# Attention scores behind all of q: three in a row, the third in the banks of the results, with the last outer product's inner products in another order

## The chip, the core and the metric

The kernel runs on one core of a Trainium2 chip. The metric is the time of one execution on the device in microseconds (us); lower is better. TensorE (PE) multiplies matrices, VectorE (DVE) adds and evicts sums, ScalarE (ACT) takes the exponentials and copies, and the DMA queues move data. Matmul results land in PSUM[...].

## The reference

Two layers of the same form on an input of 8 images, 512 channels and 32 x 32 positions (S = 1024), all in float32. Each layer is a group norm, projections to q, k and v, attention with 8 heads of 64 channels, a projection of the result and the addition of the input:

```python
xn = group_norm(x, 8 groups) * gamma + beta
q, k, v = (W_qkv @ xn + b_qkv), split into 8 heads of 64 channels
attn = softmax(q . k / 8)             # 1024 x 1024 for each head
out = x + W_p @ (attn . v) + b_p
```

## The kernel before

The work is 16 jobs, one image in one layer each, taken in pairs of images. For each job TensorE computes v, then (mixed with the output projection of the job before) k and q, and then the attention. All queues are in the order in which the Python code emits the instructions. A planner clock (`advance`, `later`) decides where transfers and other small steps are slotted in.

**Projections.** The projections of q, k and of the result are products of 2 x 2 blocks computed with seven products instead of eight, and this twice, one level inside the other. The outer level has seven outer products for each projection, in the order `OUTER = (1, 2, 6, 5, 7, 3, 4)`; each of them is again seven inner products of 128 x 128 by 128 x 256, in the order `ORDER = (1, 5, 6, 2, 7, 3, 4)`. The function `chain` holds one outer product. It uses four banks, z, y, u and w (their names rotate, so a bank called vd in a profile can be the z of its chain):

- product 1 starts z, which ScalarE copies to y; product 5 starts w, which ScalarE copies to `s5` in SBUF
- product 6 adds onto z, and ScalarE copies z to u (line 413)
- product 2 adds onto y, which ScalarE evicts (line 605, or 603 without a bias)
- product 7 adds onto z, and VectorE evicts z plus `s5` (line 609, or 607)
- product 3 adds onto u, which VectorE evicts in the same way
- product 4 adds onto z, and ScalarE evicts z (line 605, or 603)

So product 7 must come behind the copy to u, and product 4 behind product 7's eviction.

`deep_phases` makes one thunk for each inner product and interleaves neighbouring outer products: outer product c begins when the one before it is at its inner product 7, and from there the two alternate. The last outer product has nobody behind it, so its last four thunks follow each other. Each outer product uses four banks, by turns the left and the right half of PSUM; the last one has the right half. Behind the evictions of products 7 and 3 one waiting outer addition (line 622, 128 x 1024) or another small step is put into VectorE's queue.

**Attention.** A job has 8 groups (four pairs of heads, two halves of the positions) of 8 steps (blocks of 128 keys), 64 steps in all. In a step, `scores` multiplies k and q on the four 64 x 64 quarters of the array into two banks (`sc`, line 764), and ScalarE takes the exponential of 128 x 1024 numbers (line 769). VectorE adds the exponentials up (`add`, lines 779 and 781). `values` multiplies the exponentials with v into two other banks (`po`, line 795). Values run `LEAD = 2` steps behind the scores. The left half of PSUM holds two `sc` tiles, the right half two `po` tiles.

**From the projections to attention.** When all but the last two inner products of q's last outer product are issued, the left half of PSUM is given to `sc`, and scores 0 and 1 are issued; then the last two inner products (3 and 4) follow, and the right half is given to `po`. Then `run` goes on with score 2, values 0, score 3, values 1 and so on. This place occurs 16 times, once for each job.

Of the kernel before, what the change touches and what calls it, by code (L numbers as in the profile page):

```python
# [33 lines left out]
LEAD = 2  # L34
# [5 lines left out]
K, V, Q, O = range(4)  # L40
FACTOR = {1: A11, 2: A12, 3: S4, 4: A22, 5: S1, 6: S2, 7: S3}
ORDER = (1, 5, 6, 2, 7, 3, 4)
OUTER = (1, 2, 6, 5, 7, 3, 4)
QT = HALF // 2
RING = 7
# [25 lines left out]
def fast_path(  # L71
# [37 lines left out]
    def advance(us):  # L109
        clock[0] += us  # L110
        due = sorted((t for t in todo if t[0] <= clock[0]), key=lambda t: t[0])
        for t in due:
            todo.remove(t)
            t[1]()

    def banks(half, use):

        if half in ps:
            ps.pop(half)[0].__exit__(None, None, None)
        turns[0] += 1  # L120
        guard = tc.tile_pool(
            name=f"ps{half}_{turns[0]}", bufs=2 if use == "two" else 1, space=PSUM,
            side=("left", "right")[half], reuse_waits="tile",
        )
        ps[half] = (guard, guard.__enter__())

    def two_banks(tag, name):
        return ps[0 if tag == "sc" else 1][1].tile([P, 2, HALF], F32, tag=tag, name=name)
# [235 lines left out]
    def right(src, t, o):  # L364

        if o in (4, 5, 6):
            return t[:, {5: 0, 6: 1, 4: 2}[o]]
        rows = 0 if o in (1, 7) else 2
        cols = slice(0, HALF) if o in (1, 2) else slice(HALF, S)
        return src[:, rows : rows + 2, cols]  # L370
# [112 lines left out]
    def sums_of_four(r, slots):  # L483

        def blk(a, b):
            return r[:, a, b * QT : (b + 1) * QT]

        def first():  # L490
            nc.vector.tensor_sub(slots[0], blk(0, 1), blk(0, 0))
            nc.vector.tensor_sub(slots[1], blk(1, 1), slots[0])

        def second():
            nc.vector.tensor_sub(slots[2], blk(1, 1), blk(0, 1))
            nc.vector.tensor_sub(slots[3], blk(1, 0), slots[1])

        return first, second

    class OutputSums:  # L500
# [6 lines left out]
        def steps(self, c):  # L507
            def first():
# [16 lines left out]
                self.at[c] = slots  # L525
                self.pair = sums_of_four(right(self.src, to[0], OUTER[c]), slots)
                self.pair[0]()
# [3 lines left out]
    def deep_phases(n, extra, outs=None, early=()):  # L531
# [4 lines left out]
        dst = {}  # L536
        chains = [(which, o) for which in ((O, K, Q) if outs else (K, Q)) for o in OUTER]
        tiles = {}
# [4 lines left out]
        def begin(c):  # L543
            which, o = chains[c]
            m = job(which)
            b, layer = jobs[m]
            if o == OUTER[0] and which != O:
                name = "k" if which == K else "q"
# [140 lines left out]
        live, parts = {}, {(0, 0): 2, (0, 1): 3, (1, 1): 2, (1, 0): 2}  # L689
        soon, outer = deque(early), deque()  # L690

        def thunk(c, j):
            def go():
                if j == 0:
                    live[c] = begin(c)
                live[c](ORDER[j])
                if ORDER[j] in (7, 3):
                    if soon:
                        soon.popleft()()
                    elif outer:  # L700
                        outer.popleft()()
                    elif extra and extra[0][0] <= c:
                        extra.popleft()[1]()
                if j == 6:
                    end(c)
                    if c + 1 == len(chains):
                        while outer:
                            outer.popleft()()
                advance(0.43)

            return go
# [32 lines left out]
    class Attention:  # L744
# [6 lines left out]
            self.steps = [(g, kc) for g in range(len(self.groups)) for kc in range(NT)]  # L751
            self.es, self.acc, self.po = {}, {}, {}

        def scores(self, i):
            n, q, k = self.n, self.q, self.k
            groups, steps, es = self.groups, self.steps, self.es
            g, kc = steps[i]
            hp, sh = groups[g]
            sc = two_banks("sc", f"sc_{n}_{i}")
            for h in range(2):  # L760
                for j in range(2):
                    r = slice(j * HD, (j + 1) * HD)
                    k0 = kc * P + h * HD
                    nc.tensor.matmul(  # L764
                        sc[h * HD : (h + 1) * HD, j, :], k[r, hp, k0 : k0 + HD],
                        q[r, hp, sh * HALF : (sh + 1) * HALF], start=True, stop=True,
                    )
            e = epool.tile([P, 2, HALF], F32, tag="e", name=f"e_{n}_{i}")
            nc.scalar.activation(e, sc, AF.Exp, scale=SCALE)  # L769
            es[i] = e  # L770
            if i > 1:
                self.add(i)

        def add(self, i):
# [102 lines left out]

        def run(self, chores):

            steps = self.steps  # L880
            self.add(1)
            for i in range(2, len(steps) + LEAD):
                if i < len(steps):
                    self.scores(i)
                self.values(i - LEAD)
                g, kc = steps[i - LEAD]
                if kc == NT - 1:
                    self.finish(g)
                    advance(0.85)
                if i in chores:  # L890
                    chores[i]()
                advance(1.71)
# [56 lines left out]
    def extend_plan(n):  # L949
        plan.extend((n, V, o) for o in ORDER)  # L950
        plan.extend((n - 1, O, o) for o in ORDER)
        plan.extend((n, which, o) for which in (K, Q) for o in OUTER)

# [148 lines left out]
    def first_plan():  # L1102
        plan.extend((0, which, o) for which in (K, Q) for o in OUTER)
        for _ in range(RING):
# [15 lines left out]
    reads, steps = norm_steps(1)  # L1120
    for n in range(-1, len(jobs)):
        last = n + 1 == len(jobs)
        outs = None
        if n >= 0:
            chores = {}

            def put(i, fn):
                while i in chores:
                    i += 1
                chores[i] = fn  # L1130

            if last:
                w = plain_weights(n)
            else:
                if n == 0:
                    first_factors(put, [(O, 0), (V, 1)])
                elif n == 1:
                    first_factors(put, [(K, 1), (Q, 1)])
                elif n == 2:
                    first_factors(put, [(O, 1)])  # L1140
                for i, (_, fn) in enumerate(extra):
                    put(2 + i, fn)
                at = (10, 19, 22, 24, 26, 28, 36, 39, 42, 45)
                if n == 0:
                    for i, fn in zip((3, 3, 4, 5, 6, 8, 10, 11, 12, 13, 15), reads):
                        put(i, fn)
                    at = (22, 30, 34, 35, 37, 38, 41, 44, 47, 50)
                for i, fn in zip(at, steps + sums(n + 1)):
                    put(i, fn)
                deep_first = deep_steps(n + 1)  # L1150
                for at, fn in zip((52, 54, 57, 59), deep_first[4:]):
                    put(at, fn)
                put(61, lambda: (extend_plan(n + 1), [fetch() for _ in range(RING)]))
            assert max(chores, default=0) < NT * len(att.groups)
            att.run(chores)
            banks(0, "one")
            banks(1, "one")
            if last:
                advance(100.0)
                advance(100.0)  # L1160
                judge()
                plain_proj(n, w)
                break
            outs = OutputSums(n)
            out_sums(n, outs)
            first = v_phase(n + 1, ORDER)
            for thunk in first[:-1]:
                thunk()
            rest = first[-1:]
            extra = deque()  # L1170
            if jobs[n][1] == 1 and jobs[n][0] + 2 < B:
                extra.append((11, lambda b=jobs[n][0] + 2: (x_tile(b), load_x(b))))
            if n == 1:
                load, bias_steps = make_out_bias(1)
                extra.append((8, load))
                extra.extend((11, fn) for fn in bias_steps)
            if n + 2 < len(jobs):
                reads, steps = norm_steps(n + 2)
                extra.extend((15, fn) for fn in reads)
        both = deep_phases(n + 1, extra, outs, deep_first[:4] if outs else ())  # L1180
        both[0]()
        rest[0]()
        if n < 0:
            later(22.0, lambda: load_x(1))
        for thunk in both[1:-2]:
            thunk()
        banks(0, "two")
        att = Attention(n + 1)
        att.scores(0)
        att.scores(1)  # L1190
        for thunk in both[-2:]:
            thunk()
        banks(1, "two")

    for half in (1, 0):
        ps.pop(half)[0].__exit__(None, None, None)
# [246 lines left out]
```

## Time and profile before

| | |
|---|---|
| time, median of three runs | 3218.36 us (3215.56 to 3218.5) |
| span of the profiled run | 3213.6 us |
| PE, DVE, ACT busy | 99%, 86%, 59% of the span |
| scores, PE L764 | 27% of the chain that ended last |
| values, PE L795 | 26% |
| exponential, ACT L769 | 1024 times 1023 ns |
| sum of exponentials, DVE L781 | 768 times 1219 ns |
| a job, from its first score to that of the next | 198.20 us |

A line of the timeline has the start in us from the span's beginning, the duration, the engine, the line of the kernel, the operation, the tile written and the tiles read, the shapes and how many instructions were merged; in brackets the idle time before it and who ended it. Each float32 inner product appears as two matmuls, each score and each values block as eight. Matmuls overlap, so the distance of two starts, and not the duration, is the price of one.

### The profile page before, as it was taken

How to read it: one execution, taken by the hardware profiler on the slowest of the kernel's cores; microseconds unless marked ns; L12 is line 12 of the kernel's file. 1: busy time of each engine (PE TensorE's matmuls, PEld its weight loads, DVE VectorE, ACT ScalarE, POOL GpSimd, SP SyncE). 2: the span in 40 equal slices, each digit the busy share in tenths (PEclk: the TensorE clock that was granted, in tenths of full speed). 3: DMA queues.
4: the chain of work that ended last, by engine and by line, in shares of the span. 5: the costliest groups of instructions: out<-in, count | busy, mean ns of one | idle time of the engine just before them, and what ended most of it. 6: DMA issues, size and time to landing. Idle time of an engine off the chain costs nothing.

```text
span 3213.6 us, 57636 instructions
## 1 busy us (share of the span) xinstructions
PE 3194.8 (99%) x22870; PEld 1850.2 (58%) x22870; DVE 2767.3 (86%) x3958; ACT 1902.4 (59%) x3038; POOL 99.4 (3%) x93
## 2 busy tenths in 40 slices
PE   9999999999999999999999999999999999999999
PEld 7366384563836638365483754837557374573843
DVE  8897998979889798897978889888897888988876
ACT  4746646466565665656656565565656656566563
POOL 0000000000000000000000000000000000000000
PEclk9999999999999999999999999999999999999999
DMA  8234272350613305033160421505216051150501
GB/s 317 96 105 129 68 213 69 93 168 22 210 27 90 89 28 158 22 105 128 31 210 15 119 67 38 147 16 144 93 45 192 16 142 43 55 130 22 173 22 42
DMA packets 149462, 313.04 MB, mean 97 GB/s; under 512 B 33864, under 2 KB 46784, under 8 KB 148160
## 3 DMA queue, kind: packets, MB, share of 16 engines
q1 hardware_dynamic: 132320, 276.77, 26.8%
q0 software_dynamic: 16864, 32.51, 6.2%
q8 instruction: 181, 2.97, 0.4%
q14 instruction: 97, 0.79, 0.1%
HBM read 224.35 MB, written 51.18 MB: 86 GB/s over the span
## 4 chain that ended last, share of the span: by engine, by line
PE 93%; DVE 5%; DMA 1%; issue 1%; ACT 0%; SPq 0%; POOL 0%; DVEq 0%
PE sc L764 27%; PE po L795 26%; PE vd L593 10%; PE zd L593 10%; PE z L462 6%; PE ud L593 4%; PE yd L593 4%; PE v L462 2%; PE y L462 2%; PE u L462 2%; DVE acc L781 1%; PE pp L733 1%; DMA x<-p 0%; DMA w<-wqkv_dram 0%; DVE w L154 0%
## 5 line engine op out<-in xcount | busy, mean ns | idle before, releaser
L769 ACT ACTIVATE e<-sc 128x1024 f32<-128x1024 f32 x1024 | 1045.9, 1023 | 582.4 <-PE sc L764 485.9
L764 PE MATMUL sc<-q,k 64*64 64x512 f32 x8192 | 1061.7, 590 | 0.0
L795 PE MATMUL po<-e,v 64*64 64x512 f32 x8192 | 1057.1, 589 | 0.0
L781 DVE TENSOR_TENSOR acc<-acc,e 128x1024 f32<-128x1024 f32 x768 | 936.3, 1219 | 57.8 <-ACT e L769 9.3
L795 PEld LDWEIGHTS po<-e,v 64*64 64x64 f32 x8192 | 313.0, 133 | 566.0 <-issue 557.5
L764 PEld LDWEIGHTS sc<-q,k 64*64 64x64 f32 x8192 | 309.7, 133 | 559.1 <-issue 545.4
L593 PE MATMUL vd<-deep,w 128*128 128x256 f32 x900 | 252.6, 380 | 1.4 <-DVE p L609 1.3
L779 DVE TENSOR_TENSOR acc<-e,e 128x1024 f32<-128x1024 f32 x128 | 156.4, 1222 | 111.3 <-ACT e L769 111.3
L593 PE MATMUL zd<-deep,w 128*128 128x256 f32 x892 | 248.4, 380 | 3.7 <-DVE p L607 2.0
L593 PEld LDWEIGHTS vd<-deep,w 128*128 128x128 f32 x900 | 170.6, 190 | 26.4 <-DVE p L609 2.5
L593 PEld LDWEIGHTS zd<-deep,w 128*128 128x128 f32 x892 | 168.9, 190 | 29.2 <-DVE p L607 3.3
L811 DVE TRANSPOSE_TENSOR_REDUCE r<-acc 128x32 f32<-128x1024 f32 x128 | 158.5, 1238 | 0.5
L636 POOL DMA_DIRECT2D x<-p x62 | 74.6, 1203 | 1971.5 <-ACT p L603 1408.9
L593 PE MATMUL vd<-os,w 128*128 128x256 f32 x420 | 118.1, 380 | 1.6 <-DVE p L609 1.5
L622 DVE TENSOR_TENSOR p<-p,p 128x1024 f32<-128x1024 f32 x94 | 114.2, 1215 | 0.0
L462 PE MATMUL z<-w,t 128*128 128x256 f32 x480 | 110.9, 379 | 0.0
L462 PE MATMUL z<-w,xn 128*128 128x256 f32 x480 | 110.1, 382 | 0.0
L413 ACT COPY ud<-vd 128x256 f32<-128x256 f32 x173 | 61.8, 357 | 77.2 <-PE vd L593 69.8
L611 ACT COPY s<-zd 128x256 f32<-128x256 f32 x173 | 64.5, 373 | 71.8 <-PE zd L593 71.7
L475 ACT COPY v<-z 128x512 f32<-128x512 f32 x32 | 18.7, 585 | 148.5 <-PE z L462 148.5
L462 PEld LDWEIGHTS z<-w,xn 128*128 128x128 f32 x480 | 90.0, 190 | 23.8 <-issue 12.2
L413 ACT COPY ud<-zd 128x256 f32<-128x256 f32 x156 | 55.7, 357 | 76.6 <-PE zd L593 75.1
(213 smaller groups left out, 4058.7 us busy)
## 6 DMA issues: line engine op xcount, KB each, us to landing
w<-deep SPq DMA_DIRECT2D x287, 448.0 KB, 3.9
w<-keep SPq DMA_DIRECT2D x129, 256.0 KB, 2.7
x<-p POOLq DMA_DIRECT2D x62, 512.0 KB, 6.9
rb<-rd SPq DMA_DIRECT2D x96, 256.0 KB, 4.1
deep<-w SPq DMA_DIRECT2D x42, 448.0 KB, 4.0
x<-x_dram SPq DMA_DIRECT2D x28, 512.0 KB, 4.6
out_dram<-x SPq DMA_DIRECT2D x28, 512.0 KB, 6.2
keep<-raw SPq DMA_DIRECT2D x5, 1792.0 KB, 7.6
```

The source lines that it names most:

```text
L413: nc.scalar.copy(u, z)
L462: nc.tensor.matmul(ps[:, ti * CH : (ti + 1) * CH], r[:, cc, t0 : t0 + P], w[:, cc, :], start=(start and ti == 0 and cc == 0), stop=(cc == ...
L593: nc.tensor.matmul(ps, lhs[:, FACTOR[i], :], moving[i], start=start, stop=True, skip_group_check=True,)
L611: return chain(product, lambda ps: nc.scalar.copy(s5, ps), put, z, y, u, w)
L622: outer.append(lambda: nc.vector.tensor_add(to_, a, b))
L636: nc.gpsimd.dma_start(to_, p(part), accum_op=ALU.add)
L764: nc.tensor.matmul(sc[h * HD : (h + 1) * HD, j, :], k[r, hp, k0 : k0 + HD], q[r, hp, sh * HALF : (sh + 1) * HALF], start=True, stop=True,)
L769: nc.scalar.activation(e, sc, AF.Exp, scale=SCALE)
L779: nc.vector.tensor_add(acc[g], self.es[i - 1], e)
L781: nc.vector.tensor_add(acc[g], acc[g], e)
L795: nc.tensor.matmul(po[g][j * HD : (j + 1) * HD, h, :], v[r, kc, d0 : d0 + HD], e[r, j, :], start=(kc == 0), stop=(kc == NT - 1),)
L811: nc.vector.tensor_reduce(self.r[:, 0, m, :], self.acc.pop(g).rearrange("p j (b e) -> p (j b) e", e=RP), AX.X, ALU.add, apply_transpose=True,)
```

## The change

The two products of q that stood behind scores 0 and 1 are put in front of them. After q is complete, three scores are issued in a row. The left half of PSUM has room for two, so the third takes the first of the two `po` tiles in the right half, and `run` begins with values 0 and goes on with score 3. TensorE then changes only once from products of 128 rows to products of 64 rows, where it changed there, back and there again.

With the scores gone from between product 7 and product 4, the last outer product gets an order of its own, `LAST_ORDER`, which moves product 7 in front of product 2. All other outer products keep `ORDER`.

```diff
+LAST_ORDER = (1, 5, 6, 7, 2, 3, 4)
...
-                live[c](ORDER[j])
-                if ORDER[j] in (7, 3):
+                order = LAST_ORDER if c + 1 == len(chains) else ORDER
+                live[c](order[j])
+                if order[j] in (7, 3):
...
-        def scores(self, i):
+        def scores(self, i, tag="sc"):
...
-            sc = two_banks("sc", f"sc_{n}_{i}")
+            sc = two_banks(tag, f"sc_{n}_{i}")
...
-            if i > 1:
+            if i > 2:
                 self.add(i)
...
             self.add(1)
-            for i in range(2, len(steps) + LEAD):
+            self.add(2)
+            self.values(0)
+            if 2 in chores:
+                chores[2]()
+            for i in range(3, len(steps) + LEAD):
...
-        for thunk in both[1:-2]:
+        for thunk in both[1:]:
             thunk()
         banks(0, "two")
         att = Attention(n + 1)
         att.scores(0)
         att.scores(1)
-        for thunk in both[-2:]:
-            thunk()
         banks(1, "two")
+        att.scores(2, "po")
```

## The prediction

> **What bounds the kernel now.** I read the page first, for the busy engine and for the chain that ended last.
>
> ```profile
> PE 3194.8 (99%) x22870; PEld 1850.2 (58%) x22870; DVE 2767.3 (86%) x3958; ACT 1902.4 (59%) x3038; POOL 99.4 (3%) x93
> ...
> PE 93%; DVE 5%; DMA 1%; issue 1%; ACT 0%; SPq 0%; POOL 0%; DVEq 0%
> ```
>
> TensorE is busy 99% of the span and carries 93% of the chain. So only two things count: how densely TensorE's instructions follow one another, and whether one of them waits. The windows by stage say the same of one job, from its first score to the next job's:
>
> ```profile
> 888.90:1087.10 198.20, 198.20 (x1434) 115.93 (x1433) 170.70 (x237) 119.25 (x192) 6.22 (x5) 1.00 0.29 78
> ```
>
> PE is busy 198.20 of 198.20 us at a granted clock of 1.00. The change touches the place where a job's projections end and its attention begins, 16 times in a run. I read one of them in the timeline, first TensorE alone (start, duration, instruction):
>
> ```profile
> 887.05 0.59 PE L593 MATMUL vd<-deep,w 128*128 128x256 f32 x2
> 887.48 0.59 PE L593 MATMUL zd<-deep,w 128*128 128x256 f32 x2
> 887.92 0.59 PE L593 MATMUL yd<-t,w 128*128 128x256 f32 x2
> 888.35 0.59 PE L593 MATMUL vd<-deep,w 128*128 128x256 f32 x2
> 888.87 1.95 PE L764 MATMUL sc<-q,k 64*64 64x512 f32 x16
> 890.75 0.70 PE L593 MATMUL ud<-t,w 128*128 128x256 f32 x2
> 891.29 0.59 PE L593 MATMUL vd<-deep,w 128*128 128x256 f32 x2
> 891.81 1.09 PE L764 MATMUL sc<-q,k 64*64 64x512 f32 x8
> 892.72 1.04 PE L795 MATMUL po<-e,v 64*64 64x512 f32 x8
> 893.58 0.61 PE L764 MATMUL sc<-q,k 64*64 64x512 f32 x4
> ```
>
> By the chain's order these are: product 6 of q's last outer product, product 4 of the one before it, then products 2 and 7 of the last, scores 0 and 1, products 3 and 4, score 2, values 0. (In the last outer product the bank named vd is the running sum z.) Starts count here, since durations overlap. Products follow at 0.43 us, a score or a values block takes 0.86 (892.72 to 893.58). From product 2 at 887.92 to values 0 at 892.72 are 4.80 us; four products and three scores at these rates would be 4 x 0.432 + 3 x 0.859 = 4.30. The other 0.50 is at the changes of shape and nowhere else. All 16 such places have the same spacing, within 0.01 us.
>
> Then VectorE and ScalarE in the same stretch:
>
> ```profile
> 886.39 0.48 DVE L609 SCALAR_TENSOR_TENSOR p<-zd,bias_step,s 128x256 f32<-128x256 f32 x1 [0.53 <-PE zd L593]
> 886.79 1.22 DVE L622 TENSOR_TENSOR p<-p,p 128x1024 f32<-128x1024 f32 x1
> 887.92 0.48 DVE L609 SCALAR_TENSOR_TENSOR p<-ud,bias_step,s 128x256 f32<-128x256 f32 x1
> 888.32 1.22 DVE L622 TENSOR_TENSOR q<-p,p 128x1024 f32<-128x1024 f32 x1
> 889.45 0.48 DVE L609 SCALAR_TENSOR_TENSOR p<-vd,vec_sb,s 128x256 f32<-128x256 f32 x1
> 889.85 1.22 DVE L622 TENSOR_TENSOR q<-q,p 128x1024 f32<-128x1024 f32 x1
> ```
>
> ```profile
> 887.68 0.36 ACT L413 COPY ud<-vd 128x256 f32<-128x256 f32 x1 [0.49 <-PE vd L593]
> 888.12 0.47 ACT L605 ACTIVATE p<-zd,bias_step 128x256 f32<-128x256 f32 x1
> ```
>
> The 889.45 line is the eviction of product 7. Product 7 was issued at 888.35, and its eviction starts 1.1 us later because VectorE has no gap from 886.39 on: two evictions and two additions of 1.22 us stand ahead of it. In the kernel before this delay is free, because scores 0 and 1 lie between product 7 and product 4.
>
> **What the Trainium skill says.** "TensorEngine Tiling (Array Packing)", Key Properties: a change of tiling mode drains TensorE. The trace agrees and gives the price: going from 128-row products to 64-row scores costs 0.09 at once and 0.05 more after the first half of the score, 0.14 us; going back costs 0.11 and then 0.11 more before product 3's second half, 0.21 us. "PSUM — Partial Sum Buffer", Engine vs sequencer instructions: ScalarE's and VectorE's queues are strict FIFO, and matmuls start and complete in program order. The VectorE lines above agree. "TensorE: Matmul & The Clock Gate", Part 2: weight loads are pulled ahead of running matmuls. After a wait there is nothing to hide the load behind, and the trace shows that too, in the first job's outer products:
>
> ```profile
> 74.54 0.48 DVE L609 SCALAR_TENSOR_TENSOR p<-zd,vec_sb,s 128x256 f32<-128x256 f32 x1
> ...
> 75.07 0.70 PE L593 MATMUL zd<-deep,w 128*128 128x256 f32 x2 [0.93 <-DVE p L609]
> ...
> 75.61 0.59 PE L593 MATMUL yd<-xn,w 128*128 128x256 f32 x2
> ```
>
> The product that waits for an eviction starts 0.05 us after it ends (74.54 + 0.48 = 75.02, then 75.07), and the next follows at 0.54 instead of 0.43: a wait costs 0.11 on top of its length.
>
> **The change part by part.**
>
> *Scores moved behind all of q.* It removes one trip from products to scores and back: 0.14 + 0.21 = 0.36 us saved at each place (0.358 with the third digit kept).
>
> *Product 7 before product 2.* It now follows directly on the other outer product's product 4, at 887.92 if nothing held it. It adds onto z, and must not start before ScalarE has copied z to u: 887.68 + 0.36 = 888.04, so 888.10 with the 0.05. That is 0.18 of waiting and 0.11 for the load. Behind it on TensorE is everything else: product 2 at 888.63, product 3 at 889.07, product 4 due at 889.50.
>
> *Product 4 without the scores in front.* It adds onto z again, so it has to wait until product 7's eviction has read z. The four lines of VectorE's queue ahead of that eviction (outer sums and evictions of the outer product before) depend on nothing that moves, and their order is the same in both kernels. So the eviction again runs from 889.45 to 889.93; product 7 itself is done long before. Product 4 starts at 889.98, 0.48 later than due. Since this wait ends at a time that VectorE sets, it swallows the wait of product 7: the end is the same whether that one happens or not.
>
> *From there on.* Product 4 takes 0.54 after its wait, the change of shape 0.09: score 0 at 890.61. Two scores in a row take 1.77 (1.88 from 888.87 to 890.75, less the 0.11 of the way back): score 2 at 892.38, values 0 at 893.24. Before it was 892.72. The loss is 0.52 us at each place; with the third digit my sum over the 16 places is 8.3 us.
>
> *The third score in a results bank, and the waits this adds.* Score 2 needs two banks that the last outer product used, values 0 the other two, and values 0 also the first exponential. The eviction of product 3 follows the 889.85 addition and ends at about 891.5; that of product 4, on ScalarE, starts some 0.4 us after its second half and ends at about 891.2; both are ahead of 892.38. The exponential of score 0 starts 1.16 us after the score (888.87 to 890.03), so at 891.77, and ends at 892.79, ahead of 893.24. Scores 3 and 4 find their banks free since values 0 and 1 have already waited for the same exponentials. One more waiting instruction on TensorE's queue finds its condition met: I take 0, and at most 0.05 each (the restart above), 0.8 us in all.
>
> *The rest at nothing.* The additions to the sums of exponentials keep their order on VectorE; VectorE, 171 of 198 us busy, has its slack in the attention that follows. The planner's clock loses one step of 1.71, but no transfer or addition changes its place in any queue.
>
> **Rivals.**
> - *All hidden.* If copy and eviction each came half a microsecond sooner than I read, neither wait would show and only the saved change of shape would remain: 16 x 0.36 = 5.7 less, 3212.6 us, which is 0.18% and within the bound of no change. For it speaks that this is the change's purpose; against it the gapless VectorE lines.
> - *Only product 7's wait is real.* If the eviction alone comes 0.5 us sooner (an addition shorter or moved), the price is 0.18 + 0.11 - 0.36 = -0.07, or -1.2 us in all: 3217.2.
> - *A further wait behind the scores.* If values 0 had to wait for a whole exponential of 1.02 us besides, each place would lose 1.54: 24.6 us, 3243. Against it speak margins of 0.4 us and more.
>
> **How the numbers follow.** Forecast: 3218.36 + 8.3 = 3226.7 us, 0.26% slower, chance 0.77. All hidden 0.08, only product 7's wait 0.08, further wait 0.07. The range leaves out the first and the last of these rivals (0.15): from 3217.0, where the second lies, to 3231.0, the forecast with the 0.8 for queue entries and the 2.9 us by which the three runs before differ. Slower by over 0.2% means over 3224.8. The forecast is only 1.9 above, so I give some of its 0.77 to no change: slower 0.75, same 0.20, faster 0.05 (all hidden together with a low run).
>
> **What would show it.** In the trace after, the product ahead of score 0 must start 0.05 us after VectorE's eviction of vd ends and be the place of an idle gap of TensorE, product 7 must show a short wait on ScalarE's copy, and scores 0, 1 and 2 must follow at about 0.9 us with a single change of shape. A job should take 198.7 us instead of 198.2. I am wrong if product 4 starts without a wait, if product 7's eviction stands elsewhere in VectorE's queue, or if values 0 or score 2 waits for an exponential or an eviction.

## The result and the profile after

The changed kernel takes 3268.18 us (median of six runs) against 3215.39 us for the kernel before on the same chip: 1.0166 times as long, with a 95% interval from 1.0153 to 1.0179. The forecast was 3226.7 us. So the direction was right and the size was not: 8.3 us more were forecast, 52.8 came.

Line numbers of the changed kernel and of the experiments are a few higher than those of the kernel before (a score is L766 where it was L764). The page of the changed kernel, in the two rows that were shown of before (PEld is TensorE's loading of weights):

```profile
PE 3212.7 (98%) x22870; PEld 1857.3 (57%) x22870; DVE 2767.5 (85%) x3958; ACT 1903.3 (58%) x3038; POOL 99.5 (3%) x93
...
PE 70%; DVE 23%; issue 5%; DMA 2%; ACT 1%; DVEq 0%; SPq 0%; ACTq 0%
```

The number of instructions and VectorE's busy time are unchanged. But VectorE, which carried 5% of the chain that ended last, now carries 23%. One job, from its first score to that of the next, takes 201.10 us where it took 198.20 (windows by stage: stretch, its length, the busy time of PE, PEld, DVE, ACT and POOL, then the granted clock of TensorE, the DMA share and GB/s):

```profile
1117.97:1319.07 201.10, 198.65 (x1431) 115.87 (x1430) 170.67 (x237) 119.33 (x191) 6.22 (x5) 1.00 0.29 77
```

**The place that the prediction worked on** came out as forecast. TensorE there, in the timeline of the changed kernel:

```profile
1115.45 0.70 PE L594 MATMUL vd<-deep,w 128*128 128x256 f32 x2
1115.99 0.59 PE L594 MATMUL yd<-t,w 128*128 128x256 f32 x2
1116.42 0.59 PE L594 MATMUL ud<-t,w 128*128 128x256 f32 x2
1117.34 0.70 PE L594 MATMUL vd<-deep,w 128*128 128x256 f32 x2 [0.33 <-DVE p L610]
1117.97 2.81 PE L766 MATMUL sc<-q,k 64*64 64x512 f32 x24
1120.60 1.04 PE L797 MATMUL po<-e,v 64*64 64x512 f32 x8
```

And ScalarE and VectorE:

```profile
1115.05 0.36 ACT L414 COPY ud<-vd 128x256 f32<-128x256 f32 x1 [0.49 <-PE vd L594]
1115.68 1.21 DVE L623 TENSOR_TENSOR q<-p,p 128x1024 f32<-128x1024 f32 x1
1116.81 0.47 DVE L610 SCALAR_TENSOR_TENSOR p<-vd,vec_sb,s 128x256 f32<-128x256 f32 x1
1117.21 1.21 DVE L623 TENSOR_TENSOR q<-q,p 128x1024 f32<-128x1024 f32 x1
```

Product 7 (1115.45) has waited for the copy of z, which ends at 1115.41: the next start comes 0.54 later, as after a wait, and not 0.43. Product 4 (1117.34) starts when the eviction of product 7 is over (1116.81 + 0.47 = 1117.28, and 0.06); it was due 0.43 after 1116.42. The eviction itself stands behind the same addition as before. Then come 24 matmuls of three scores in a row, with one change of shape. The loss here is 0.52 us, taken between the same VectorE instructions in both kernels: one ahead of the place, the other 20 us and more behind it.

**The rest is 112 us further on**, where the attention ends and v of the next job begins. The list of who waited for whom has one new entry at its head for TensorE (total, times, longest):

```profile
PE z L463 <- DVE q L820: 34.9, 15, 4.4
```

TensorE in that place, in the timeline of the changed kernel:

```profile
1226.17 1.90 PE L797 MATMUL po<-e,v 64*64 64x512 f32 x16
1228.00 1.99 PE L463 MATMUL z<-w,xn 128*128 128x256 f32 x8
1232.10 1.99 PE L463 MATMUL z<-w,xn 128*128 128x256 f32 x8 [2.11 <-DVE q L820]
```

VectorE in the same stretch:

```profile
1228.97 1.22 DVE L783 TENSOR_TENSOR acc<-acc,e 128x1024 f32<-128x1024 f32 x1
1230.23 1.25 DVE L813 TRANSPOSE_TENSOR_REDUCE r<-acc 128x32 f32<-128x1024 f32 x1
1231.39 0.65 DVE L820 TENSOR_TENSOR q<-po,px 128x512 f32<-128x512 f32 x1
```

The first product of v in the left half runs at once. The first one in the right half waits 2.11 us until VectorE has evicted the results of the last group (1231.39 + 0.65 = 1232.04). In the kernel before TensorE goes from the left to the right half without a gap:

```profile
1196.51 1.90 PE L795 MATMUL po<-e,v 64*64 64x512 f32 x16
1198.33 3.72 PE L462 MATMUL z<-w,xn 128*128 128x256 f32 x16
```

though VectorE's last eviction is just as late there, 4.05 us from the start of v's first product to its end (4.04 in the changed kernel):

```profile
1200.56 1.25 DVE L811 TRANSPOSE_TENSOR_REDUCE r<-acc 128x32 f32<-128x1024 f32 x1
1201.73 0.65 DVE L818 TENSOR_TENSOR q<-po,px 128x512 f32<-128x512 f32 x1
```

So VectorE has not become slower or later; it is TensorE that now depends on another eviction. The right half of PSUM holds two `po` tiles, which are taken in turn; each covers two of the half's four banks. Eight groups take eight tiles, and in the kernel before the last group has the second. In the right half the phase of v puts its z and y where the first tile was, so it waits for the eviction of group 6, long past. The third score takes one more tile at the start of the job. From there every group has the other tile, the last group has the first, and z lies on it. In the program as built, the value for which that product waits is indeed that of group 6's eviction before, and of group 7's after, in all 15 jobs that follow an attention.

### The profile page after: what moved, and what is told of

It reads as the page before. It is cut to its first block, busy times and chain, and to the rows that moved or that the text cites. A ratio compares the mean times of both kernels' runs of the same rounds, so it can differ in the third digit from the quotient of the medians.

```text
span 3273.9 us, 57578 instructions
## 1 busy us (share of the span) xinstructions
PE 3212.7 (98%) x22870; PEld 1857.3 (57%) x22870; DVE 2767.5 (85%) x3958; ACT 1903.3 (58%) x3038; POOL 99.5 (3%) x93
## 4 chain that ended last, share of the span: by engine, by line
PE 70%; DVE 23%; issue 5%; DMA 2%; ACT 1%; DVEq 0%; SPq 0%; ACTq 0%
PE sc L766 17%; PE po L797 15%; DVE acc L783 11%; PE vd L594 10%; PE zd L594 9%; PE z L463 6%; PE yd L594 4%; PE ud L594 3%; DVE acc L781 2%; PE v L463 2%; PE y L463 2%; PE u L463 1%; DVE q L820 1%; DVE r L813 1%; DVE q L874 1%
## 5 line engine op out<-in xcount | busy, mean ns | idle before, releaser
L766 PE MATMUL sc<-q,k 64*64 64x512 f32 x8192 | 1058.0, 589 | 0.0
L766 PEld LDWEIGHTS sc<-q,k 64*64 64x64 f32 x8192 | 311.3, 133 | 562.7 <-issue 545.1
L463 PE MATMUL z<-w,xn 128*128 128x256 f32 x480 | 120.1, 400 | 34.9 <-DVE q L820 34.9
L608 DVE TENSOR_TENSOR p<-vd,s 128x256 f32<-128x256 f32 x63 | 26.7, 424 | 87.6 <-PE vd L594 87.6
```

What stands on the lines that cost most here:

```text
L463: nc.tensor.matmul(ps[:, ti * CH : (ti + 1) * CH], r[:, cc, t0 : t0 + P], w[:, cc, :], start=(start and ti == 0 and cc == 0), stop=(cc == ...
L766: nc.tensor.matmul(sc[h * HD : (h + 1) * HD, j, :], k[r, hp, k0 : k0 + HD], q[r, hp, sh * HALF : (sh + 1) * HALF], start=True, stop=True,)
```

## The experiments

Theory A is this shift of the turn. Theory B is that attention starts later, VectorE lags all through it and its end waits for the lag. Each kernel below ran beside the kernel before on one chip; e1 to e4, e5 to e8 and e9 had three different chips. Across these groups only the differences from the kernel before are compared.

**e1: the pairs of banks exchanged in v's right half.**

```diff
-            z, y, u, w = (bank(i, b, f"{b}_{which}_{n}_{i}") for b in "zyuv")
+            tags = "uvzy" if i == 1 and n > 0 else "zyuv"
+            t = {b: bank(i, b, f"{b}_{which}_{n}_{i}") for b in tags}
+            z, y, u, w = (t[b] for b in "zyuv")
```

> The changed kernel, with one difference: in the first phase after an attention (v of the next job) the bank pairs z, y and u, v of the right half change places, so that the first product of v lands on the results tile that was used last but one again. Theory A (the third score shifts the turn of the two results tiles, and v's first product in the right half then waits for the last eviction): the wait of some 2.4 us behind each of 15 attentions goes away, 3215.4 + 8.3 = 3223.7 us (3222 to 3226), and the granted clock stays at 1.00. Theory B (attention starts later, VectorE lags all through it and the end waits for it): no difference from the changed kernel, about 3268.

Measured: 3225.08 us against 3216.7, ratio 1.0026 (1.0016 to 1.0036), that is 8.4 us. A steady job, by the windows:

```profile
2089.05:2287.78 198.73, 198.39 (x1432) 115.96 (x1431) 170.73 (x237) 119.23 (x191) 6.22 (x5) 1.00 0.33 99
```

The kernel before has 198.21 by the same measure, from first score to first score (the 198.20 above is a window cut at two digits). 198.73 less 198.21 is the 0.52 of the place alone. The 15 waits of z on the last eviction are gone from the list, and TensorE goes from the left to the right half without a gap again:

```profile
2199.08 3.72 PE L465 MATMUL z<-w,xn 128*128 128x256 f32 x16
```

Theory B falls, since attention begins just as late here.

**e2: the same exchange in the kernel before.**

> The kernel before, with the same exchange of bank pairs in the phase of v, and nothing else: now v's first product in the right half lands on the results tile used last. Theory A: 15 waits of about 2.37 us appear, 35.6 us, and some half-rate stretches of TensorE's clock with them: 3251 at least, about 3260. Theory B: nothing changes, 3215.

Measured: 3265.78 us against 3216.7, ratio 1.0156 (1.0140 to 1.0172), with none of the changes of the diff in it: 49.1 us more, where the expectation has about 45. Its list of waits has the entry of the changed kernel again:

```profile
PE z L464 <- DVE q L820: 35.1, 15, 4.5
```

So the wait comes with the bank alone, without a third score and without a later start of attention.

**e3: the old order of the last outer product, with e1's banks** (`order = ORDER` for all).

> As e1, but the last outer product keeps the order 1 5 6 2 7 3 4. If VectorE's queue alone sets when product 4 may start (its eviction of product 7 stands behind two additions), the order of 7 and 2 makes no difference: 3223.7, within 1 us of e1. If TensorE's own order sets it, product 7 is done 0.25 us later than in e1 and each of 16 places loses as much: 4 us more than e1.

Measured: 3224.61 us, ratio 1.0025 (1.0016 to 1.0034); a steady job 198.73, equal to e1. The order of 7 and 2 is worth nothing as long as VectorE sets when product 4 may start.

**e4: the addition ahead of product 7's eviction put behind it.** This is e1 with one more edit.

```diff
                     elif outer:
-                        outer.popleft()()
+                        if c + 2 < len(chains) or order[j] != 3:
+                            outer.popleft()()
```

> As e1, but the outer addition that stands directly ahead of product 7's eviction in VectorE's queue is put behind it (and one behind product 3's eviction likewise). If that addition makes product 4 wait, product 7's short wait for the copy (0.18 + 0.11) remains against 0.36 saved: 0.07 less than before at each of 16 places, 3214.3, that is 9.4 us less than e1. If the wait has another cause, it is as e1, 3223.7.

Measured: 3216.93 us, ratio 1.0002 (0.9994 to 1.0011), 8.2 us less than e1 and level with the kernel before. A steady job takes 198.14, which is 0.07 less than before, as worked out. In its timeline product 4 (2079.63) follows product 3 at 0.43, and the eviction is over in time (2078.97 + 0.48 = 2079.45):

```profile
2078.23 0.70 PE L596 MATMUL vd<-deep,w 128*128 128x256 f32 x2
2078.97 0.48 DVE L612 SCALAR_TENSOR_TENSOR p<-vd,vec_sb,s 128x256 f32<-128x256 f32 x1 [0.43 <-PE vd L596]
2079.20 0.59 PE L596 MATMUL ud<-t,w 128*128 128x256 f32 x2
2079.63 0.59 PE L596 MATMUL vd<-deep,w 128*128 128x256 f32 x2
```

Some 1.3 us are missing from the forecast; the first job has a stop of 1.37 us of TensorE, the same as in e5.

**e5: the last eight products woven anew, with e4's held addition.** The last outer product has the old `ORDER` here; the weaving alone separates its products.

```diff
         at = sorted((7 * c + 2 * j, c, j) for c in range(len(chains)) for j in range(7))
+        tail = at[-8:]
+        at[-8:] = [tail[i] for i in (0, 2, 1, 4, 5, 3, 6, 7)]
```

> As e4, with the last eight inner products woven anew: 5, 6 of the last outer product, 3 of the one before, 2, 7, then 4 of the one before, 3, 4. Product 7 now has two products behind the 6 whose copy it needs, and product 4 has two behind the 7 whose eviction it needs. If copy and eviction are all that held TensorE, no wait is left and only the saved change of shape remains: 16 x 0.358 = 5.7 us less than before, 3211.0 (3210 to 3212.5), faster than both kernels. If the order of the products has a price of its own, it stays at e4's 3217.

Measured: 3213.93 us against 3217.22, ratio 0.9990 (0.9982 to 0.9999). A steady job takes 197.85, 0.36 less than before, which is the whole price of the saved change of shape. TensorE in the timeline (products 7, 4 of the other, 3, 4, then the scores):

```profile
889.44 0.60 PE L596 MATMUL vd<-deep,w 128*128 128x256 f32 x2
889.88 0.59 PE L596 MATMUL zd<-deep,w 128*128 128x256 f32 x2
890.31 0.59 PE L596 MATMUL ud<-t,w 128*128 128x256 f32 x2
890.74 0.59 PE L596 MATMUL vd<-deep,w 128*128 128x256 f32 x2
891.26 2.81 PE L771 MATMUL sc<-q,k 64*64 64x512 f32 x24
```

and VectorE:

```profile
889.45 0.48 DVE L612 SCALAR_TENSOR_TENSOR p<-ud,bias_step,s 128x256 f32<-128x256 f32 x1
890.08 0.48 DVE L612 SCALAR_TENSOR_TENSOR p<-vd,vec_sb,s 128x256 f32<-128x256 f32 x1
890.48 1.22 DVE L625 TENSOR_TENSOR q<-p,p 128x1024 f32<-128x1024 f32 x1
```

The products keep their 0.43 throughout; product 7's eviction now comes 0.64 after its start, ends at 890.56 and is 0.18 ahead of product 4. Of 5.7 us the run brought 3.3. The first job has a new stop, in the timeline of e5 on ScalarE:

```profile
103.40 1.15 ACT L248 ACTIVATE xn<-x,off 128x1024 f32<-128x1024 f32 x1 [1.75 <-DVE off L245]
...
104.55 1.00 ACT L776 ACTIVATE e<-sc 128x1024 f32<-128x1024 f32 x1
```

The squares of the second image's norm (L248) wait for a 0.15 us step of VectorE (L245), and the exponential queued behind them keeps TensorE for 1.37 us. That step stands later in VectorE's queue than in e1: behind the next group's first sum, a reduction and an eviction, and no longer ahead of them. By the code, other small steps that found no place among the products, because of the held additions, move into the attention and push it back.

**e6: e4 with the old order.**

> As e4, with the order 1 5 6 2 7 3 4 kept. With VectorE free, product 7's time counts: 7 starts at its old place, its eviction ends 1.22 us later, product 4 is due 0.86 after it and waits 0.41 + 0.11; less the 0.36 saved that is 0.16 a place, 2.6 us more than before and 2.5 to 3.5 more than e4: about 3219.5. If the order of 7 and 2 never matters, it is equal to e4.

Measured: 3219.82 us, ratio 1.0010 (1.0002 to 1.0019). The sum fits, but for a wrong reason: a steady job takes 198.27, only 0.06 more than before and not 0.16, and the first job has the stop of e5 here too, which makes up most of the rest. I had let the eviction begin 0.74 after product 7's start, which is so after a wait; without one it is the 0.64 seen in e5. The new order, worth nothing in e3, is worth 0.13 a job once VectorE is free.

**e7: two idle products put into the wait of the changed kernel.**

```diff
-            for thunk in first[:-1]:
+            first[0]()
+            for i in range(2):
+                idle_products(0, "u", f"fill_{n}_{i}")
+            for thunk in first[1:-1]:
                 thunk()
```

> The changed kernel as it is, with two idle products of 128x512 (about 0.86 us each, on a bank that is free and written again before it is read) put into TensorE's queue between the first and the second thunk of v, where it waits some 2.4 us. If the waits also cost by letting the granted clock fall to half for 3.4 us at a time, the fall goes away and the time is 3216.7 + 8.4 + 35.6 = 3260.7, 6 to 9 us less than the changed kernel, with runs closer together. If the clock plays no part, it stays at 3268.

Measured: 3264.44 us against 3217.22, ratio 1.0148 (1.0132 to 1.0163): 47.2 us more than before instead of the changed kernel's 52.8, though a steady job takes the same 201.1. In the profile of the changed kernel, TensorE's clock is granted at half for 3.41 us at seven places, five of them right behind such a wait. One of them, by the windows:

```profile
203.68:207.09 3.41, 3.41 (x10) 2.70 (x9) 3.28 (x9) 0.57 (x1) 0.00 (x0) 0.50 0.00 0
```

With the wait filled, 10.2 us of half rate are left, all in the first 210 us, where the changed kernel has 23.9. The clocks of all runs give the same picture: the granted clock is 0.996 to 0.998 in the six runs of the changed kernel, lowest in the two longest, and 0.999 in three of the four runs here (0.998 in the fourth). So the clock has a part, 5.6 us by the two differences, where 6 to 9 were expected. Which waits bring it is read from the traces in the last section.

**e8: the new order alone in the kernel before.**

> The kernel before, with the new order of the last outer product alone, scores 0 and 1 still between products 2 and 3. Product 7 waits for the copy of z, 0.18 + 0.11 at each of 16 places, and nothing else changes: 4.6 us more than before, 3221.3. If a wait for ScalarE's copy is absorbed elsewhere, it is as before, 3216.7.

Measured: 3221.26 us against 3217.22, ratio 1.0012 (1.0006 to 1.0019), 4.0 us; a steady job 198.49, 0.28 more. In its timeline product 7 is the one at 890.84, with the copy's wait in front and the bare load behind:

```profile
890.23 0.59 PE L594 MATMUL zd<-deep,w 128*128 128x256 f32 x2
890.84 0.70 PE L594 MATMUL vd<-deep,w 128*128 128x256 f32 x2
891.37 0.59 PE L594 MATMUL yd<-t,w 128*128 128x256 f32 x2
```

**e9: e5 from the second place on.** Holding and weaving are left out at the first place (`if outs:`).

> As e5, but the first of the 16 places keeps the old weaving and its additions are not held, since in e4 and e5 the first job then shows a wait of 1.4 us of TensorE for an exponential (a small VectorE step, on which ScalarE waits, came late behind the held addition), and took 2.5 to 2.9 us longer. If that is the whole of what e5 lacks of 5.7, the first place costs 0.52 as in e1, the other 15 save 0.358 each: 4.9 us less than before, about 1.5 less than e5 (3212.4 against a before of 3217.2). If the first job's loss has another cause, it stays at e5's 3.3 less.

Measured: 3211.00 us against 3215.69, ratio 0.9984 (0.9977 to 0.9990): 4.7 us less than before, against the 4.9 expected, and some 57 less than the changed kernel by the two differences. The first job takes 203.91 in its profile, 207.40 in e5's, the steady jobs are equal, and the stop is gone from its trace. So that stop was most of e5's loss. This version has the largest gain here, though its interval overlaps that of e5.

## Why the prediction was wrong

- *What bounds the kernel*: right. TensorE has nothing to spare, and its waits in the steady jobs came out in the time.
- *Scores behind all of q, one trip saved, 0.36*: right. e5 has this alone, 198.21 - 197.85.
- *Product 7's wait for the copy, 0.18 + 0.11*: right, by e8 (0.28), and swallowed by the later wait, by e3 against e1.
- *Product 4's wait for the eviction, set by VectorE's queue*: right. e4 removes it by moving one addition, and 0.52 a place is what e1 has left once the other matter is taken out (8.4 us against 8.3).
- *The third score in a results bank, and the waits this adds*: this step failed. It asked only whether score 2 and values 0 find their banks free, which they do. It did not follow the taken tile to the next who take one. Two tiles taken in turn make eight groups come out on the other tile, and the step after attention was built on the old turn. The text put that under *the rest at nothing*, and none of the rivals had it: the third, a further wait behind the scores, sought it 112 us too early. What the runs show in its place is a wait of 2.11 us at the start of v, which costs 2.37 us in each steady job. The signs that the prediction named at the place of the edit all came out; only the length of a job (198.7 forecast, 201.10 measured) spoke against it.
- *The size of it*: in the profiled runs the changed kernel takes 60.3 us more. 16 places at 0.52 are 8.3. The 14 later waits, taken at the 2.37 of a steady job (201.10 less e1's 198.73) are 33.2, and the first is 3.1 (4.4, less a wait of 1.3 that the kernel before has in the same place). Seven half-rate stretches of 3.41 lose half of themselves, 11.9; in the steady jobs the one that holds such a stretch takes 202.79 instead of 201.11. One wait for a weight block is 2.3. As an estimate that makes 58.8; the remaining 1.5 was not traced. Of the 52.8 by the medians, the two kinds of wait are 44.6. The rest fits the lower granted clock, but those runs have no trace.

The profile of before held what was needed: the last eviction ended at 1202.38, 4.05 us behind the start of v's first product (1198.33), and neither half of v's first products waited. That a queue ends late without harm is a hint to ask which buffer saves it.

## What to carry to other kernels

If a change takes one buffer more from a pool that is used in turn, count on to the end of the loop: all later users come out on the other buffer, and whoever follows the loop may land on the one that is free last. An eviction that ended late without harm then becomes a wait far away from the edit (here 2.4 us, 112 us later). And where work is taken from between two dependent steps, look at what stands ahead of the step between them in its own engine's queue: moving a 1.22 us addition, and putting two products between each dependent pair, gave back all of what the move had cost at that place.

## What the runs showed of the hardware

A wait of TensorE of 2.1 us was followed in some cases, not in all, by 3.41 us at half of the clock. "TensorE: Matmul & The Clock Gate" of the Trainium skill (Part 1, What's actually happening) names windows of 3413 ns, and half rate after at least one idle window. The length and the rate agree with the trace. The condition does not: the waits here are shorter than one such window, and the measurement decides.

Which waits bring it can be read from the traces. In each run all half-rate stretches begin on one grid of 3.413 us: in the changed kernel at 203.68, 411.89 and 620.11, for example, which are 61 steps apart. What counts is the idle time of TensorE within one interval of that grid. Here is one wait of 2.11 us that lies in one interval, and one of 2.12 us of which 0.16 falls into the next, each with the interval behind it (the idle time is the length less the first busy time, PE; the clock is the third number from the end):

```profile
616.69:620.11 3.42, 1.31 (x7) 1.08 (x7) 3.26 (x7) 0.57 (x1) 0.00 (x0) 1.00 0.01 2
620.11:623.52 3.41, 3.41 (x10) 2.69 (x9) 3.28 (x10) 0.57 (x1) 0.00 (x0) 0.50 0.14 48
1831.83:1835.24 3.41, 1.47 (x7) 0.95 (x5) 3.27 (x4) 0.76 (x2) 0.00 (x0) 1.00 0.00 0
1835.24:1838.66 3.42, 3.25 (x15) 2.89 (x16) 3.20 (x12) 0.57 (x1) 0.00 (x0) 1.00 0.11 18
```

In the eleven traces, leaving out the first 7 us and the last microseconds, all 15 intervals with 1.996 us or more of idle time are followed by half rate (seven in the changed kernel, six in e2, two in e7). Of the 60 with 1.0 to 1.98 us two are: one in e1 with 1.86, and one in e2 with 1.57 that was itself at half rate. So a limit near 2.0 us in one interval fits these runs; the first of these two exceptions stays open. A job of 201.10 us is not a whole number of steps of 3.413, so the same wait lies elsewhere on the grid in each job, and only some of them bring a stretch. The kernel before, whose waits in steady jobs are nil, has no such stretch before its last microseconds.
